# First chunk of a state-space block: D * u as products with a diagonal, modulation products one ahead of their sums, row statistics and transposes tile by tile, the feed-forward gate moved into the loop

## The chip, the core and the metric

One NeuronCore of a Trainium2 chip runs the kernel. The metric is the device time of one execution in microseconds. The core has five instruction queues that run in parallel and wait for one another through semaphores: TensorE (PE: matrix products and transposes into PSUM), VectorE (DVE), ScalarE (ACT), GpSimd (POOL) and SyncE (SP, which here issues all the DMAs). Each queue runs its own instructions strictly in the order in which the program wrote them.

## The reference

Two blocks follow each other on x (2 batches, 2048 rows, 512 features), both in float32. Only the first one is touched here. It is an S5 state-space layer with modulation by a condition t, followed by a feed-forward layer:

```python
mod = t @ Wm + bm
shift_a, scale_a, gate_a, shift_ff, scale_ff, gate_ff = jnp.split(mod, 6, axis=-1)
y_mod = _ln(y) * (1 + scale_a[:, None]) + shift_a[:, None]
a_y = _s5(y_mod, ...)       # 2 * Re(C xs) + D_diag * u, xs[l] = Lam_bar * xs[l-1] + B_bar u[l]
y = y + gate_a[:, None] * a_y
scale_c, shift_c = jnp.split(t @ Wc + bc, 2, axis=-1)
y_norm = _ln(y) * (1 + scale_c[:, None]) + shift_c[:, None]
y_mod = y_norm * (1 + scale_ff[:, None]) + shift_ff[:, None]
h = jax.nn.gelu(y_mod @ W1 + b1)
return y + gate_ff[:, None] * (h @ W2 + b2)
```

The second block is a style layer norm with softmax attention (16 heads) and a residual. It takes most of the time and stays as it is.

## The kernel before, in words

x is worked in chunks of 512 rows: 2 batches by 4 chunks. A chunk is four tiles of 128 rows (rows on the partitions, 512 features along them). For products over features it is transposed into four pieces of 128 features by 512 rows. Every float32 product is two instructions on TensorE; a transpose is one.

The order of the work is written out by hand; nothing reorders it. There is a prologue, which does everything of the first chunk up to its feed-forward product (L243 to L601), and then a loop over the chunks (L628). Each turn of the loop runs the feed-forward products of one chunk (`ff_first` L484 and `ff_second` L495, 16 steps f), and a table `due[f, half]` hangs the other work between them: the state-space part of the next chunk and the attention projections of the one before. In the first turn two steps stand in that table beside these: `rest_of_mod` (L616, two more modulation vectors) and `rows_of_biases` (L624).

The prologue, in order:

- SP loads x, the weights of the modulation vectors (1 MB each, `load_mod` L215), B (`br`, `bi`), C (`c2_re`, `c2_im`), and the feed-forward weights in quarters.
- VectorE computes the constants of the state-space layer on one column (128x1): `exp_full` (L286) for the step and for the decay, sine and cosine, and then the scaled B (`bb_re`, `bb_im`, L377). Most are short operations that depend on the one before. POOL multiplies C by 2 and -2 (L381).
- `modulate` (L220) makes a modulation vector: TensorE multiplies the condition with the weights in four column groups (tile `pq`, L226), ScalarE copies the result (`quarters`, L230), and TensorE sums the four groups with small products (L233). For several vectors this chain is done one after another: product, copy, sum. `modulated` (L235) adds the biases on VectorE.
- `normalised` (L392) takes the layer norm of the chunk: statistics of all four tiles, scale, then four normalising operations. `to_features` (L145) transposes the normalised chunk by feature piece, four tiles each, and ScalarE applies scale and shift.
- `phases` (L341) builds the rotation table by doubling on VectorE. `s5_in` (L415) multiplies with B (`pu`), `s5_turn` (L425) rotates, `s5_scan` (L437) runs the recurrence (two scans) and rotates back into `h_re`, `h_im`; in the last two POOL does one operation and three operations.
- `s5_direct` (L456) adds D * u, times the gate, on POOL: u is the normalised chunk with a scale and a shift, so the rows `r_scale` and `r_shift` multiply and are added, three operations a tile. `gate_row` (L387) spreads such a vector over all partitions by TensorE and a copy.
- `s5_out` (L464): for each tile the two products with C (`pa`), the gate on VectorE (`gated`), the addition to x on POOL.
- `gate_row` for the feed-forward gate and its bias, then the second layer norm (`ff_norm` L476, in which POOL also adds the gated bias b2), and its transposes (`ff_features` L481).

PSUM has eight banks: two buffers with the tag `ph`, four banks with the tag `po`, and two banks that `ones` gives out in turn.

Of the kernel before, what the change touches and what calls it, by code (L numbers as in the profile page):

```python
# [39 lines left out]
def tile_s5_block_then_sln_attention(  # L40
# [87 lines left out]
    def ln_stats(src, n, mean, rstd):  # L128

        mv = small.tile([P, n, 2], F32, name="ln_mv", tag=f"ln_mv{n}")  # L130
        for t in range(n):
            st = small.tile([P, 6], F32, name="ln_st", tag="ln_st", bufs=4)
            nc.vector.bn_stats(st, src[:, t, :])
            nc.vector.bn_aggr(mv[:, t, :], st)
        v = small.tile([P, n], F32, name="ln_v", tag=f"ln_v{n}")
        nc.vector.tensor_scalar(v, mv[:, :, 1], EPS, None, ALU.add)
        nc.vector.tensor_copy(mean, mv[:, :, 0])
        rsqrt(v, rstd, n)
# [81 lines left out]
    def modulate(pm, *ms, first=0):  # L220

        for i, m in enumerate(ms, first):
            w = wms.pop(m)
            pq = ps1.tile([P, D], F32, name="pq", tag="ph")
            for k in range(KC):
                nc.tensor.matmul(  # L226
                    pq[32 * k : 32 * k + 32, :], cond_q[:, k, :], w[:, k, :], start=True, stop=True
                )
            quarters = work1.tile([P, D], F32, name="quarters", tag="hid", bufs=3)
            nc.scalar.copy(quarters, pq)  # L230
            for f in range(KC):
                at = slice((i * KC + f) * NB, (i * KC + f + 1) * NB)
                nc.tensor.matmul(pm[:, at], quarters[:, f * P : (f + 1) * P], four, start=True, stop=True)  # L233

# [14 lines left out]
    c2_im = s5c.tile([P, D], F32, name="c2_im")  # L249
    for dst, src in ((br, b_re), (bi, b_im), (c2_re, c_reT), (c2_im, c_imT)):  # L250
        nc.sync.dma_start(dst, src)
# [4 lines left out]
    load_mod(SHIFT_C, xlate, "x1")  # L256
    load_mod(GATE_F, xpool, "x2")
    w1_sb = wts.tile([P, KC, FC * P], F32, name="w1_sb")
    w2_sb = wts.tile([P, FC, D], F32, name="w2_sb")
    for q in range(4):  # L260
        f = FC // 4
        cols = slice(q * f * P, (q + 1) * f * P)
        nc.sync.dma_start(w1_sb[:, :, cols], w1[:, cols].rearrange("(k p) f -> p k f", p=P))
        nc.sync.dma_start(w2_sb[:, q * f : (q + 1) * f, :], w2[cols, :].rearrange("(c p) e -> p c e", p=P))


    def col(name):
        return s5c.tile([P, 1], F32, name=name)

    def ts(dst, a, s1, s2, op0, op1=None):  # L270
        if op1 is None:
            nc.vector.tensor_scalar(dst, a, s1, None, op0)
        else:
            nc.vector.tensor_scalar(dst, a, s1, s2, op0, op1)

    def stt(dst, a, s, b, op0, op1):
        nc.vector.scalar_tensor_tensor(dst, a, s, b, op0, op1)

    def poly(dst, r, cs):

        ts(dst, r, cs[-1], None, ALU.mult)
        for c in reversed(cs[1:-1]):
            stt(dst, dst, c, r, ALU.add, ALU.mult)
        ts(dst, dst, cs[0], None, ALU.add)

    def exp_full(dst, a, n):  # L286

        q, k, r = col(f"{n}q"), col(f"{n}k"), col(f"{n}r")
        ts(q, a, 88.0, -87.0, ALU.min, ALU.max)
        ts(k, q, LOG2E, ROUND, ALU.mult, ALU.add)  # L290
        ts(k, k, ROUND, None, ALU.subtract)
        stt(r, k, -LN2_HI, q, ALU.mult, ALU.add)
        stt(r, k, -LN2_LO, r, ALU.mult, ALU.add)
        poly(dst, r, [1.0, 1.0, 1 / 2, 1 / 6, 1 / 24, 1 / 120, 1 / 720, 1 / 5040])
        e = s5c.tile([P, 1], I32, name=f"{n}e")
        ts(e, k, 127.0, 8388608.0, ALU.add, ALU.mult)
        nc.vector.tensor_mul(dst, dst, e.bitcast(F32))

# [4 lines left out]
    nc.vector.tensor_mul(theta, l_im, dt)  # L303
    exp_full(decay, damp, "dc")

# [70 lines left out]
    bb_im = s5w.tile([P, D], F32, name="bb_im", tag="m5")  # L376
    ts(bb_re, br, k_re, None, ALU.mult)  # L377
    stt(bb_re, bi, neg_im, bb_re, ALU.mult, ALU.add)
    ts(bb_im, br, k_im, None, ALU.mult)
    stt(bb_im, bi, k_re, bb_im, ALU.mult, ALU.add)  # L380
# [27 lines left out]
    def tag_of(b, c):  # L408
        return f"f{index[b, c] % 2}"
# [14 lines left out]

    def s5_turn(b, c):  # L425

        bu = bus.pop((b, c))
        m = [s5w.tile([P, CH], F32, name=f"m{i}") for i in range(6)]
        nc.vector.tensor_mul(m[0], bu[0], t_re)
        nc.vector.tensor_mul(m[3], bu[0], t_im)  # L430
        nc.vector.tensor_mul(m[1], bu[1], t_im)
        nc.vector.tensor_mul(m[2], bu[1], t_re)  # L432
        nc.vector.tensor_add(m[0], m[0], m[1])
        nc.gpsimd.tensor_tensor(m[2], m[2], m[3], ALU.subtract)  # L434
        bus[b, c] = m

    def s5_scan(b, c):  # L437
        m = bus.pop((b, c))
# [5 lines left out]
        nc.vector.tensor_mul(m[0], m[1], t_re)  # L444
        nc.gpsimd.tensor_mul(m[4], m[1], t_im)
        nc.vector.tensor_mul(m[2], m[3], t_im)
        nc.gpsimd.tensor_mul(m[5], m[3], t_re)
        nc.vector.tensor_sub(h_re, m[0], m[2])
        nc.gpsimd.tensor_tensor(h_im, m[4], m[5], ALU.add)
        for i, h in enumerate((h_re, h_im)):  # L450
# [103 lines left out]
    def s5_gates(b):  # L554
        gate_row(b, "r_scale", r_scale)
        gate_row(b, "r_shift", r_shift)
        gate_row(b, "gate_a", mod[:, GATE_A])

# [3 lines left out]
    for dst, src in ((bT_re, bb_re), (bT_im, bb_im)):  # L562
# [3 lines left out]
        nc.scalar.copy(dst.rearrange("p k q -> p (k q)"), pb)  # L566
    modulate(spare[:, 1], GATE_A)
    normalised(*start)
    modulated(spare[:, 0], SHIFT_A, SCALE_A)
    nc.vector.tensor_scalar(u_scale, mod[:, SCALE_A], 1.0, None, ALU.add)  # L570
    for k in range(KC):
        s5_features(*start, k)
    modulated(spare[:, 1], GATE_A)
    nc.vector.tensor_mul(r_shift, mod[:, GATE_A], per_feature(V_D))
    nc.vector.tensor_mul(r_scale, r_shift, u_scale)
    nc.vector.tensor_mul(r_shift, r_shift, mod[:, SHIFT_A])
    phases()
    later = (SHIFT_F, SCALE_F, SCALE_C, SHIFT_C, GATE_F)
    modulate(spare[:, 2], *later[:1])
    s5_gates(start[0])  # L580
    s5_in(*start)
    modulate(spare[:, 2], *later[1:], first=1)
    s5_direct(*start, (0, 1))
    s5_turn(*start)
    s5_direct(*start, (2,))
    s5_scan(*start)
    s5_direct(*start, (3,))
    modulated(spare[:, 2], *later)
    tmp = small.tile([P, KC, NB], F32, name="zs")
# [3 lines left out]
    nc.vector.tensor_add(z_shift, z_shift, mod[:, SHIFT_F])  # L593
    nc.vector.tensor_mul(gate_b2, mod[:, GATE_F], per_feature(V_B2))
    for t in range(TT):
        s5_out(*start, t)
    gate_row(start[0], "gb2", gate_b2)
    gate_row(start[0], "gate_f", mod[:, GATE_F])
    ff_norm(*start)
    for k in range(KC):  # L600
        ff_features(*start, k)  # L601

# [10 lines left out]
    bv_row = wlate.tile([P, D], F32, name="bv_row")  # L613
    bp_row = wlate.tile([P, D], F32, name="bp_row")

    def rest_of_mod():  # L616
# [11 lines left out]
    for i, now in enumerate(order):  # L628
# [8 lines left out]

        if i == 0:
            due[1, 1].append((rest_of_mod,))
            due[2, 1].append((rows_of_biases,))  # L640
        if behind:
# [682 lines left out]
```

## Time and profile before

| what | us |
|---|---|
| median of 3 runs | 3458.43 (3457.08 to 3461.29) |
| the profiled execution, its own time | 3459.56 |
| its span, first to last instruction | 3457.8 |
| prologue, to the first product of the feed-forward (L487) | 80.45 |
| from there to the end of the first eight products of its third step | 24.6 (80.45 to 105.02) |
| TensorE busy in the prologue | 56.8 of 80.45 |
| TensorE busy from 117 to 860 us (rest of the feed-forward stretch read) | 742.7 of 742.9 |

Busy shares of the whole span mix stages with different limits, so the prologue is read by its chain of waits and by its timeline. In a row of the timeline stand start, length, engine, line, operation, the tile written, the tiles read, and how many instructions were merged; a bracket gives the idle time of the engine before it and what ended that time. The row of a window also names the TensorE clock that was granted (1.00 is the full clock), and the share of time in which the DMA engines were busy.

### The profile page before, as it was taken

The page shows a single profiled execution, that of the slowest core. Times are in us where ns is not written, and L with a number is a line of the kernel's source. Part 1 is how long each engine was busy: PE and PEld are TensorE (multiplying, and loading weights), DVE is VectorE, ACT ScalarE, POOL GpSimd, SP SyncE. Part 2 cuts the span into 40 slices and gives each one's busy share as a digit, 9 for nine tenths or more (in the row PEclk, how much of TensorE's full clock was granted, in tenths as well). Part 3 has the DMA queues.
Part 4 walks back from the last instruction along what each step waited for, and adds up shares of the span by engine and source line. Part 5 has one row for each costly group of instructions (what it writes and reads, how often), then busy time and mean ns, then how long its engine had stood idle before and what let it go on. Part 6 is the DMA issues. An engine that isn't in the chain of part 4 may idle for free.

```text
span 3457.8 us, 34348 instructions
## 1 busy us (share of the span) xinstructions
PE 3335.5 (96%) x11764; PEld 1508.3 (44%) x11764; DVE 2151.7 (62%) x2976; ACT 1939.8 (56%) x2208; POOL 2137.8 (62%) x1162
## 2 busy tenths in 40 slices
PE   7999999999999999999999999999999999999997
PEld 4444444444444444444444444444444444444432
DVE  6232323232322310688888888888888888888885
ACT  2111111111111111398999999999888888888963
POOL 4133131313131310289898989998898989899986
PEclk8999999999999999999999999999999999999999
DMA  8001111111110112432223222223234233233233
GB/s 304 1 31 43 43 43 43 43 43 43 43 43 31 43 37 61 121 77 67 58 62 72 66 67 54 72 67 75 70 81 96 65 87 85 71 85 78 61 97 115
DMA packets 201396, 237.06 MB, mean 69 GB/s; under 512 B 89544, under 2 KB 118728, under 8 KB 197126
## 3 DMA queue, kind: packets, MB, share of 16 engines
q1 hardware_dynamic: 201222, 234.87, 24.5%
q8 instruction: 93, 1.52, 0.2%
q14 instruction: 81, 0.66, 0.1%
HBM read 166.77 MB, written 67.76 MB: 68 GB/s over the span
## 4 chain that ended last, share of the span: by engine, by line
PE 73%; DVE 14%; ACT 8%; issue 2%; DMA 1%; POOL 1%; SPq 0%; DVEq 0%; ACTq 0%; POOLq 0%
PE o L834 15%; PE ph L487 13%; PE po L500 13%; PE s L754 10%; DVE run L770 10%; PE pk L530 6%; ACT x L765 4%; PE pv L542 3%; PE m L779 3%; PE py L905 2%; PE pt_run L790 2%; ACT pT L824 2%; ACT x L824 2%; PE pu L421 2%; PE pt_tf L149 1%
## 5 line engine op out<-in xcount | busy, mean ns | idle before, releaser
L813 POOL TENSOR_TENSOR x<-x,shift 128x1024 f32<-128x1024 f32 x704 | 1653.8, 2387 | 153.6 <-DMA shift<-flat 104.6
L765 ACT COPY x<-s 128x1024 f32<-128x1024 f32 x704 | 692.4, 1012 | 213.0 <-PE s L754 211.9
L770 DVE TENSOR_TENSOR run<-s,run 128x1024 f32<-128x1024 f32 x576 | 702.9, 1220 | 73.6 <-ACT x L765 50.2
L824 ACT ACTIVATE x<-x 128x1024 f32<-128x1024 f32 x704 | 739.8, 1060 | 11.9 <-POOL x L813 11.6
L754 PE MATMUL s<-qs,ks 128*128 128x512 f32 x2048 | 669.5, 421 | 51.3 <-DVE run L770 45.2
L834 PE MATMUL o<-x,v 128*64 128x512 f32 x2816 | 718.4, 612 | 0.0
L487 PE MATMUL ph<-fT,w_sb 128*128 128x512 f32 x1024 | 463.5, 597 | 0.0
L500 PE MATMUL po<-w_sb,hid 128*128 128x512 f32 x1024 | 460.3, 592 | 0.0
L754 PEld LDWEIGHTS s<-qs,ks 128*128 128x128 f32 x2048 | 334.4, 189 | 275.4 <-DVE run L770 149.7
L819 DVE TENSOR_TENSOR pT<-s,shift 128x1024 f32<-128x1024 f32 x320 | 389.5, 1217 | 85.1 <-PE s L754 85.1
L784 DVE TENSOR_REDUCE top<-m 128x1 f32<-128x640 f32 x512 | 417.4, 815 | 9.8 <-PE m L779 7.1
L491 ACT ACTIVATE hid<-ph,vec 128x512 f32<-128x512 f32 x128 | 88.0, 687 | 595.9 <-PE ph L487 595.9
L824 ACT ACTIVATE pT<-pT 128x1024 f32<-128x1024 f32 x320 | 339.4, 1061 | 50.2 <-DVE pT L819 50.2
L158 DVE SCALAR_TENSOR_TENSOR lo<-pk,vec,hi 128x512 fp32r<-128x512 f32 x64 | 48.0, 751 | 494.4 <-ACT hi L157 494.4
L834 PE MATMUL o<-pT,v 128*64 128x512 f32 x1280 | 330.5, 595 | 7.9 <-ACT pT L824 7.9
L487 PEld LDWEIGHTS ph<-fT,w_sb 128*128 128x128 f32 x1024 | 193.3, 192 | 228.9 <-issue 228.9
L834 PEld LDWEIGHTS o<-x,v 128*64 128x64 f32 x2816 | 157.1, 135 | 310.4 <-issue 191.4
L434 POOL TENSOR_TENSOR m<-m,m 128x512 f32<-128x512 f32 x8 | 13.1, 1643 | 449.7 <-DVE m L432 449.7
L500 PEld LDWEIGHTS po<-w_sb,hid 128*128 128x128 f32 x1024 | 190.7, 190 | 221.5 <-issue 221.5
L779 PE MATMUL m<-ks,qs 128*128 128x320 f32 x1024 | 256.6, 332 | 17.3 <-DVE top L784 15.5
L157 ACT ACTIVATE hi<-pk,vec 128x512 fp32r<-128x512 f32 x64 | 44.0, 687 | 383.3 <-PE pk L530 383.3
L510 POOL TENSOR_TENSOR x<-x,gated 128x512 f32<-128x512 f32 x32 | 39.6, 1269 | 354.4 <-DVE gated L509 354.4
(253 smaller groups left out, 2774.6 us busy)
## 6 DMA issues: line engine op xcount, KB each, us to landing
ks<-kd SPq DMA_DIRECT2D x128, 256.0 KB
qs<-qd SPq DMA_DIRECT2D x512, 64.0 KB
shift<-flat SPq DMA_DIRECT2D x64, 512.0 KB
x<-in_x SPq DMA_DIRECT2D x8, 1024.0 KB
w_sb<-in_w SPq DMA_DIRECT2D x8, 1024.0 KB
x<-x SPq DMA_DIRECT2D x8, 1024.0 KB
kd<-hi SPq DMA_DIRECT2D x32, 256.0 KB
kd<-lo SPq DMA_DIRECT2D x32, 256.0 KB
```

Source lines behind the costliest of these rows:

```text
L487: nc.tensor.matmul(ph, w1_sb[:, k, f * P : (f + 1) * P], fts[b, c][:, k, :], start=k == 0, stop=k == KC - 1)
L500: nc.tensor.matmul(pos[b, c][:, t, :], hid[:, t * P : (t + 1) * P], w2_sb[:, f, :], start=f == 0, stop=f == FC - 1,)
L530: nc.tensor.matmul(pk, w[:, k, g * P : (g + 1) * P], hT[:, k, :], start=k == 0, stop=k == KC - 1)
L754: nc.tensor.matmul(s[:, e, :], kst[pair_of[n], e][:, kt * P : (kt + 1) * P], qst[n][:, e, :], start=True, stop=True,)
L765: nc.scalar.copy(x, s)
L770: nc.vector.tensor_tensor(runs[n], s, kept[n, 0] if kt == 1 else runs[n], ALU.max)
L779: nc.tensor.matmul(m[:, i, :YW], qst[n][:, e, t * P : (t + 1) * P], kst[pair_of[n], e][:, k : k + YW], start=True, stop=True,)
L784: nc.vector.tensor_reduce(tops[n][:, j, 0:1], m[:, :, :YW], AX.XY, ALU.max, negate=True)
L813: nc.gpsimd.tensor_tensor(x, x, shifts[n], ALU.add)
L819: nc.vector.tensor_tensor(x, s, shifts[n], ALU.add)
L824: nc.scalar.activation(x, x, AF.Exp)
L834: nc.tensor.matmul(outs[n][64 * e : 64 * e + 64, :], v[:, kt, e : e + 2, :], x[:, e, :], start=first, stop=final,)
```

## The change

- The exponential of the decay (15 operations) moves from VectorE to POOL. The operations that took a scalar and a column are written as one tensor-scalar operation each.
- `br` times a column goes from VectorE to ScalarE (two operations), ahead of everything else that ScalarE does.
- `modulate` issues the product of the next vector before the sum of the last one. The vectors are grouped anew: SHIFT_A and SCALE_A as before; GATE_A, SHIFT_F and SCALE_F together; SCALE_C and SHIFT_C together; GATE_F goes into the loop.
- The loads of C move behind the weights of the modulation vectors, the one of GATE_F behind the first two quarters of the feed-forward weights.
- In the first chunk the operations that POOL had in `s5_turn` and `s5_scan` are VectorE's. Later chunks keep them on POOL.
- In the first chunk `s5_direct` is gone: D * u is added in PSUM, by 16 products of u with diagonal tiles (`direct`, made by POOL), ahead of the products with C. The rows `r_scale` and `r_shift`, which later chunks still need, move into the loop.
- The statistics of the second layer norm follow each tile's addition, the last tile's addition is VectorE's, and the transposes go tile by tile into one four-bank PSUM tile.
- Three steps hang in the loop's first turn: `gate_of_feed_forward` at (1, 0), with the vector GATE_F, its two rows and POOL's addition of the gated bias; `rest_of_mod` at (1, 1), as before; the rows of `s5_gates` at (2, 0).

```diff
@@ modulate
+        def sums(i, quarters):
+            for f in range(KC):
+                at = slice((i * KC + f) * NB, (i * KC + f + 1) * NB)
+                nc.tensor.matmul(pm[:, at], quarters[:, f * P : (f + 1) * P], four, start=True, stop=True)
...
             nc.scalar.copy(quarters, pq)
-            for f in range(KC):
-                at = slice((i * KC + f) * NB, (i * KC + f + 1) * NB)
-                nc.tensor.matmul(pm[:, at], quarters[:, f * P : (f + 1) * P], four, start=True, stop=True)
+            if behind:
+                sums(*behind)
+            behind = i, quarters
+        sums(*behind)
@@ loads
-    for dst, src in ((br, b_re), (bi, b_im), (c2_re, c_reT), (c2_im, c_imT)):
+    for dst, src in ((br, b_re), (bi, b_im)):
...
-    load_mod(GATE_F, xpool, "x2")
+    for dst, src in ((c2_re, c_reT), (c2_im, c_imT)):
+        nc.sync.dma_start(dst, src)
...
+        if q == 0:
+            load_mod(GATE_F, xpool, "x2")
@@ constants
-    exp_full(decay, damp, "dc")
+    exp_full(decay, damp, "dc", nc.gpsimd)
...
-    ts(bb_re, br, k_re, None, ALU.mult)
+    nc.scalar.activation(bb_re, br, AF.Identity, scale=k_re)
+    nc.scalar.activation(bb_im, br, AF.Identity, scale=k_im)
     stt(bb_re, bi, neg_im, bb_re, ALU.mult, ALU.add)
-    ts(bb_im, br, k_im, None, ALU.mult)
@@ first chunk
-    modulate(spare[:, 1], GATE_A)
+    modulate(spare[:, 1], GATE_A, SHIFT_F, SCALE_F)
...
+    uT = fts[start]
+    s5_in(*start)
+    modulated(spare[:, 1], GATE_A, SHIFT_F, SCALE_F)
     phases()
...
-    s5_gates(start[0])
-    s5_in(*start)
-    modulate(spare[:, 2], *later[1:], first=1)
-    s5_direct(*start, (0, 1))
-    s5_turn(*start)
-    s5_direct(*start, (2,))
-    s5_scan(*start)
-    s5_direct(*start, (3,))
+    modulate(spare[:, 2], SCALE_C, SHIFT_C)
+    s5_turn(*start, nc.vector)
+    gate_row(start[0], "gate_a", mod[:, GATE_A])
+    s5_scan(*start, nc.vector)
+
+    direct = work1.tile([P, KC, P], F32, name="direct", tag="hi")
+    for k in range(KC):
+        nc.gpsimd.tensor_scalar(direct[:, k, :], ident, vec[:, V_D + k : V_D + k + 1], None, ALU.mult)
+    pas = [ps1.tile([P, CH], F32, name="pa_s", tag="ph") for _ in range(2)]
+    pas += [ones.tile([P, CH], F32, name="pa") for _ in range(2)]
+    for t, pa in enumerate(pas):
+        cols = slice(t * P, (t + 1) * P)
+        for k in range(KC):
+            nc.tensor.matmul(
+                pa[:, k * P : (k + 1) * P], uT[:, k, cols], direct[:, k, :], start=k == 0, stop=False
+            )
...
+    for t, pa in enumerate(pas):
+        cols = slice(t * P, (t + 1) * P)
+        nc.tensor.matmul(pa, h_re[:, cols], c2_re, start=False, stop=False)
+        nc.tensor.matmul(pa, h_im[:, cols], c2_im, start=False, stop=True)
+    for t, pa in enumerate(pas):
+        g = work1.tile([P, D], F32, name="gated")
+        nc.vector.tensor_mul(g, pa, gate[start[0], "gate_a"])
+        if t:
+            ln_row(xc, t - 1, mv)
+        (nc.gpsimd if t < TT - 1 else nc.vector).tensor_tensor(xc[:, t, :], xc[:, t, :], g, ALU.add)
+    ln_row(xc, TT - 1, mv)
+    ln_scale(mv, TT, mean, rstd)
...
     for t in range(TT):
-        s5_out(*start, t)
-    gate_row(start[0], "gb2", gate_b2)
-    gate_row(start[0], "gate_f", mod[:, GATE_F])
-    ff_norm(*start)
+        normalise(xn[:, t, :], xc[:, t, :], mean, rstd, t)
+        for k in range(KC):
+            nc.tensor.transpose(pt[:, k, t * P : (t + 1) * P], xn[:, t, k * P : (k + 1) * P], ident)
     for k in range(KC):
-        ff_features(*start, k)
+        nc.scalar.activation(
+            fts[start][:, k, :], pt[:, k, :], AF.Identity,
+            bias=z_shift[:, k, start[0] : start[0] + 1], scale=z_scale[:, k, start[0] : start[0] + 1],
+        )
@@ the loop's first turn
+    def gate_of_feed_forward():
+        pm = ones.tile([P, KC * NB], F32, name="pg")
+        modulate(pm, GATE_F)
+        modulated(pm, GATE_F)
+        nc.vector.tensor_mul(gate_b2, mod[:, GATE_F], per_feature(V_B2))
+        gate_row(start[0], "gb2", gate_b2)
+        gate_row(start[0], "gate_f", mod[:, GATE_F])
+        for t in range(TT):
+            nc.gpsimd.tensor_tensor(xc[:, t, :], xc[:, t, :], gate[start[0], "gb2"], ALU.add)
...
         if i == 0:
+            due[1, 0].append((gate_of_feed_forward,))
             due[1, 1].append((rest_of_mod,))
+            due[2, 0].append((s5_gates, start[0]))
             due[2, 1].append((rows_of_biases,))
```

## The prediction

> **What bounds the kernel now.** I read the shares per engine and the chain of waits first: they ask whether a microsecond won at the front reaches the end.
>
> ```profile
> PE 3335.5 (96%) x11764; PEld 1508.3 (44%) x11764; DVE 2151.7 (62%) x2976; ACT 1939.8 (56%) x2208; POOL 2137.8 (62%) x1162
> PE 73%; DVE 14%; ACT 8%; issue 2%; DMA 1%; POOL 1%; SPq 0%; DVEq 0%; ACTq 0%; POOLq 0%
> ```
>
> TensorE is busy 96% of the span. In the feed-forward stretch from 117 to 860 us it is busy 742.7 of 742.9 us: no slack is left there to absorb an earlier start, so what the front gains passes on. The diff touches the front, up to the first feed-forward product (L487, 80.45 us), and three steps inside that loop's first turns. So I read the chain of the first 120 us next (start, length, what).
>
> ```profile
> 35.08 6.87 PE pu L421 x16
> 41.95 1.04 PE pq L226 x8
> ...
> 51.00 1.87 PE spare L233 x8
> 52.87 1.91 PE pq L226 x8
> 54.85 0.59 ACT quarters L230
> 55.49 1.86 PE spare L233 x8
> 57.35 1.92 PE pa L469 x2
> ...
> 66.41 0.87 PE pa L470 x2
> ...
> 67.38 0.69 DVE gated L472
> 68.07 0.61 DVE ln_st L133
> ...
> 73.48 3.82 DVE xn L141 x4
> ...
> 80.66 8.41 PE ph L487 x16
> ```
>
> TensorE sets the order to 67.3: four modulation vectors from 41.95 to 57.35, each a product (pq), a wait for ScalarE's copy, a sum (spare); then the output products pa. After that VectorE sets it. The last scan value, h_im, is there at 55.65 (its last copy is at 55.68), so VectorE and POOL trail TensorE closely.
>
> Third, the clock by half microseconds, since one product costs 1.04 or 1.9 us by it (columns: window, length, PE busy, clock, DMA share, GB/s).
>
> ```profile
> 28.50:29.00 0.50, 0.50 (x4) 0.50 1.04 385
> 29.00:29.50 0.50, 0.50 (x8) 0.99 1.06 389
> ...
> 46.00:46.50 0.50, 0.00 (x0) 0.58 1.06 393
> 46.50:47.00 0.50, 0.49 (x3) 0.50 1.04 385
> ```
>
> The changes, at 25.6, 29.0, 46.1, 63.1, 73.4, 83.6 and 97.3, lie whole multiples of 3.41 us apart: the clock is decided per window. My reading of the windows: dense products for about 85% of one raise it, under some 45% drop it, and the tiny sums (128x2) hardly count.
>
> Fourth, what POOL does to VectorE.
>
> ```profile
> 33.95 1.28 POOL L460 TENSOR_TENSOR xn<-xn,r_scale 128x512 f32<-128x512 f32 x1 [16.00 <-ACT r_scale L168]
> 34.01 1.36 DVE L272 TENSOR_SCALAR tb<-t_re,t_im 128x256 f32<-128x256 f32 x1
> 43.19 0.68 DVE L433 TENSOR_TENSOR m<-m,m 128x512 f32<-128x512 f32 x1
> 43.91 4.32 DVE L442 TENSOR_TENSOR_SCAN m<-decay,m 128x512 f32<-128x512 f32 x2
> 48.15 1.69 DVE L444 TENSOR_TENSOR m<-m,t_re 128x512 f32<-128x512 f32 x1
> ```
>
> A VectorE operation on two tensors takes 0.68 us alone (0.60 apart) and about 1.7 beside POOL's; the scan 1.20 to 2.22 over all its uses.
>
> **The change, stage by stage**, on the clock windows of this trace.
>
> *To 19 us: nothing.* The decay exponential leaves VectorE for POOL, -2.63 us (5.42 to 8.05); POOL's c2 scaling leaves this stretch, about -0.5 (k_re took 0.66 instead of 0.16). k_re is then ready near 12.7, but br lands about 13.35 (an estimate: c_re landed at 14.69, two 256 KB loads later at 390 GB/s). ScalarE makes bb_re and bb_im, 13.35 to 14.55; VectorE's two remaining operations end at 15.3 (19.0 before). But these two stand on ScalarE ahead of the first quarters copy, which moves from 11.96 to 14.6; the second product, now one ahead, waits for its megabyte until 12.65 (9.96, where the first landed, + 2.7 for 1 MB at 390 GB/s). The sums run 15.25 to 18.95, against 18.89 before. One-ahead is worth nothing here.
>
> The 15 dependent POOL operations are shown nowhere in this form. The nearest row:
>
> ```profile
> 3447.49 0.20 POOL L1090 TENSOR_TENSOR c<-scale 128x4 f32<-128x4 f32 x1
> 3447.77 0.20 POOL L1091 TENSOR_TENSOR c<-c,v 128x4 f32<-128x4 f32 x1
> ```
>
> Start to start 0.29, hence 4.3 us, done at 9.7; needed by about 11.6, that is 0.41 us each. Bounds: 0.20 (busy time alone) costs nothing; 0.60 (twice the row) costs 15 x 0.19 = 2.9. I take 0.29, nothing: VectorE's other constants cover it.
>
> *19 to 38.5: +3.4.* Transposes of bb end at 20.9. Three products and three sums, warm from about 22.2: first product 1.6, then 2 x 1.05 and 3 x 1.05, with copies hidden by one-ahead and only issue gaps: 27.75. Their weights, 1 MB each behind bi's 14.0, land at 16.7, 19.4 and 22.1, in time. The layer norm on VectorE is done at 22.8 (7.4 us after 15.3), so the 16 transposes begin at 27.75 and end at 30.8 by ScalarE's four 0.7 us passes; the clock falls at 29.0 after the sums and rises at 32.4. Input products pu (16 instructions): 30.85 to 32.4 at half clock, 1.8 of them at 0.855, then 14.2 at 0.43 = 6.1, ending 38.5 against 41.95. The r_scale and r_shift rows (16 of 24, 1.9 us) no longer stand ahead of them.
>
> Here a rule speaks against the change. The Trainium skill, "TensorE: Matmul & The Clock Gate", Part 4, says that transposes do not count as activity for the full clock. The row is against it: from 25.6 to 29.0 TensorE ran nothing but L149 transposes, and at 29.0 the clock rose. By the rule pu would stay at half speed one window longer: 3.41 / 2 = 1.7 us off the sum below, 10.9 in place of 12.6. I take the row.
>
> *38.5 to 48.7: +5.2.* Before, 15.4 us from 41.95 to 57.35 for four vectors. Now two: 4 x 1.06 = 4.25, to 42.75. That window holds little dense work, so the clock falls as at 46.1: the gate_a row 1.75, then 32 diagonal products (16 in two passes) at 0.107 warm, as in L164's 0.86 for 8, twice that cold: 1.55 cold and 2.65 warm. TensorE is ready at 48.7 (47.0 if the clock holds, 51.5 if all is cold). VectorE: phases start at 28.3 behind the later modulated, 8.1 us without POOL beside the wide steps, +0.5 for c2, end 36.9; turn waits for pu's imaginary half, 38.7 + 4 x 0.61 = 41.15; scans 2 x 1.25; six products 3.65: h_im at 47.3. POOL's c2 scaling moves behind five loads and finishes near 31.6; nothing needs it before 47. Moving POOL's share to VectorE costs 4 x 0.6 there and frees both from each other. TensorE decides, by 1.4 us.
>
> *pa, 48.7 to 55.6: +3.0.* 16 at 0.43 = 6.9 us; before 9.9, half of it at half clock. gated, row statistics and POOL's add (0.6, 0.8, 1.27) fit in each tile's 1.72.
>
> *Tail: +4.7.* Before 67.28 to 80.45 = 13.2. Now after the last pa: gated 0.7, one row's statistics 0.85, add on VectorE 0.7, last row 0.85, scale 2.3 (L134 to L141), four xn 1.92 (as at 24.43; 3.82 beside POOL's bias adds), transposes and ScalarE's first pass 1.2 = 8.5. Loop starts at 64.1: 16.3 us earlier.
>
> *Inside the loop: -3.7.* Gate of feed-forward: product 1.06, copy 0.76, sums 1.05, VectorE 0.55, two rows 1.75 = 5.2; everything on TensorE behind it, po first, waits for it. ScalarE's gelu of the second piece (0.69) stands ahead of the copy and ends within the product. Two rows of s5_gates: 1.75. Against it, rest_of_mod took 92.43 to 98.6 and left the next eight ph at half clock until 105.02: 9.2 us beyond ph's own 3.43. One ahead it is 4.2 us, too short to drop the clock for most window positions: 5.3 with 0.38 x 3. The same for the gate step, 0.2 x 3 = 0.6. Sum 5.8 + 1.75 + 5.3 - 9.2 = 3.7. POOL's bias adds, 5.1 us, find POOL idle from 80 to 154; uncovered they would add 1.9 to the tail, as before.
>
> SP's queue: GATE_F goes behind two weight quarters, landing near 37, needed at 73 (14.0 + 8.5 MB at 2.7). x1, wk and the rest wait for modulation products that are now earlier.
>
> **Sum** 3.4 + 5.2 + 3.0 + 4.7 - 3.7 = 12.6. Other window positions can only add cold stretches to the gate row and triple; estimate -0.8. Gain 11.8. On the profiled execution (span 3457.8, 1.76 around it, 3459.56) that is 3447.8; it lies 1.1 above the median 3458.43, which gives 3446.6. I say **3447**. Under 0.2% (7 us) is what a measurement cannot tell from no change.
>
> **The rivals.**
> - *The clock takes it back* (13%). Bad window positions: triple +1.5, pu +1.7, gate row and diagonals +1.5, ph behind both loop steps +3.5: gain about 4, 3454. For: the clock fell twice beside such steps. Against: they are shorter now.
> - *Clock holds throughout* (15%). pu one us earlier, diagonals 1.7 earlier but VectorE's 47.3 decides (+1.4), loop +1.7: gain 16, 3442.
> - *Nothing arrives* (5%): a later wait absorbs it, 3457. Against: 742.7 of 742.9.
> - *POOL's exponential becomes the bound* (5%). At L297 for decay: ScalarE's bb_re waits for k_re, the quarters copies wait behind it, TensorE's sums behind those. Price 15 x (p - 0.41) us: the gain is gone at p = 1.2, slower by 7 us at p = 1.66: 3465. For: operations with a pointer scalar on POOL are not in the trace. Against: 0.29.
>
> **How the numbers follow.** The forecast has 62%, its own range 3443 to 3451. Faster: 62 + 15 = 77%; same: 13 + 5 = 18%; slower 5%. The range 3441 to 3454 takes in the holding clock and the bad one; outside lie mostly the last two rivals and errors of my schedule.
>
> **What would show it.** Right: the first ph near 64 us; pa beginning within 1 us of h_im and of the last diagonal product; scans near 1.25 us, L444 near 0.68; xn 0.5 each. Wrong: decay's last POOL operation after 11.6 and the first quarters copy after 14.6; the transposes behind the triple later than 30; a half clock during pa or through the second ph; po's first product more than 6 us behind the second ph.

## The result, and the profile after

The changed kernel takes 3445.73 us (median of 6 runs, 3444.56 to 3452.13), the kernel before 3459.61 us in the same comparison (6 runs, 3457.08 to 3465.84). The ratio is 0.9961, 95% interval 0.9948 to 0.9974: 13.9 us less. The forecast was 3447 us, about 11.8 us less.

First the engines' shares and the chain by engine, on the page of the changed kernel.

```profile
PE 3325.6 (97%) x11796; PEld 1506.7 (44%) x11796; DVE 2141.9 (62%) x2964; ACT 1940.9 (56%) x2210; POOL 2119.3 (62%) x1164
PE 73%; DVE 13%; ACT 9%; DMA 2%; issue 2%; POOL 1%; SPq 1%; DVEq 0%; ACTq 0%; POOLq 0%
```

As before, TensorE sets the time; it has 32 instructions more (the diagonal products). Next the chain of waits of its first 100 us (start, length, what).

```profile
13.41 1.28 ACT L393
14.71 0.72 ACT bb_re L393
...
20.14 1.81 PE pb L582 x8
21.95 3.49 PE pq L238 x16
...
33.58 8.05 PE pu L437 x16
41.63 1.85 PE pq L238 x16
43.49 1.88 PE spare L231 x16
...
48.15 1.79 PE pa L607 x16
49.94 0.86 PE pa_s L623 x2
...
56.84 0.69 DVE gated L627
...
62.68 3.67 PE pt_s L639 x16
66.42 0.79 ACT fT L641
67.25 7.13 PE ph L503 x16
74.39 1.04 PE pq L238 x8
...
86.94 3.54 PE ph L503 x8
...
97.48 3.44 PE ph L503 x8
```

The last row is the mark that all runs below are read by: the first feed-forward product of the loop's fourth step. By then everything that the change touches is done, the steps moved into the loop included. In the kernel before it is this row:

```profile
110.24 3.44 PE ph L487 x8
```

It stands at 110.24 before and at 97.48 after: **12.76 us** earlier, against 12.6 in the forecast's sum. The first attention products (tile m) start at 1398.7 and 1386.0, 12.7 apart: what is gained at the mark arrives undiminished 1300 us later. From there to the end it takes 2059.1 us before and 2057.3 after, and between 2056.7 and 2062.5 over all the profiles below, so that a total holds a few microseconds that no part of the change has made.

| where | before | forecast | after |
|---|---|---|---|
| transposes of bb begin | 18.76 | 18.95 | 20.00 |
| pu ends | 41.95 | 38.5 | 41.63 |
| first pa | 57.35 | 48.7 | 49.94 |
| last pa ends | 67.28 | 55.6 | 56.82 |
| first ph | 80.45 | 64.1 | 67.25 |
| mark, ph of the fourth step | 110.24 | 97.6 | 97.48 |

The total is right, the way there is not: the prologue gained 13.2 us instead of 16.3, and the loop gave back 0.4 instead of 3.7.

### The profile page after: what moved, and what is told of

The parts are those of the page before. It is cut to its first block, busy times and chain, and to the rows that moved or that the text cites. A ratio compares the mean times of both kernels' runs of the same rounds, so it can differ in the third digit from the quotient of the medians.

```text
span 3443.3 us, 34398 instructions
## 1 busy us (share of the span) xinstructions
PE 3325.6 (97%) x11796; PEld 1506.7 (44%) x11796; DVE 2141.9 (62%) x2964; ACT 1940.9 (56%) x2210; POOL 2119.3 (62%) x1164
## 4 chain that ended last, share of the span: by engine, by line
PE 73%; DVE 13%; ACT 9%; DMA 2%; issue 2%; POOL 1%; SPq 1%; DVEq 0%; ACTq 0%; POOLq 0%
PE o L892 15%; PE ph L503 13%; PE po L516 13%; PE s L812 10%; DVE run L828 9%; PE pk L546 6%; ACT x L823 4%; PE pv L558 3%; PE m L837 3%; PE py L963 2%; PE pt_run L848 2%; ACT pT L882 2%; ACT x L882 2%; PE pu L437 2%; PE pt_tf L155 1%
```

## The experiments

Beside each total stands the ratio to the kernel before, timed on the same chip. Totals that differ by less than 3 us can't be told apart by a handful of runs; the mark comes from one profiled execution of each.

### The yardstick: the changed kernel once more

> The changed kernel once more, as a yardstick on the same chip for the runs beside it: 3444 to 3448 us, the first feed-forward product at 66 to 69 us, the fourth step at 96.5 to 99.

Measured: 3448.22 us, ratio 0.9964 (0.9951 to 0.9976), first ph 67.12, mark 97.35. The mark repeats within 0.13 us, the median within 2.5 us. That the mark repeats so closely is luck, as the runs below show: in six executions TensorE has the same work up to the end of pu (these two, the run with the clock held, the two with POOL's share, and the one with the gate behind the output products), and pu ends at 41.63, 41.60, 40.61, 39.49, 39.23 and 38.47. The changes of the clock lie elsewhere in each execution. A difference of less than 3 us between the marks of two profiles is therefore not shown to come from the edit.

### One-ahead undone

```diff
-            if behind:
-                sums(*behind)
-            behind = i, quarters
-        sums(*behind)
+            sums(i, quarters)
```

> The changed kernel with each modulation vector's sums issued directly behind its own product again, the one-ahead order undone everywhere, all else kept. Theory: nothing in the first pair (the quarters copies wait behind bb on ScalarE in both), two exposed copies of about 0.75 us each in the group of three, one in the group of two and one in the loop's pair, and more half clock: first feed-forward product 2.5 to 4 us later, near 70 to 71 us, the loop's pair of vectors 4.5 us or more and not 3.7, total 3 to 6 us longer than the changed kernel. Rival, VectorE's rotation and scan set the start of the output products: the first feed-forward product is less than 1 us later.

Measured: 3458.65 us, ratio 0.9998 (0.9989 to 1.0006), first ph 75.00, mark 110.23. The whole gain is gone, four times my lower bound and twice the upper. The chain of this run:

```profile
16.64 1.87 PE spare L231 x8
18.51 1.91 PE pq L238 x8
20.44 0.60 ACT quarters L242
21.08 1.86 PE spare L231 x8
22.94 1.81 PE pb L579 x8
...
40.19 7.27 PE pu L434 x16
...
95.46 1.86 PE pm L231 x8
97.32 5.90 PE ph L500 x8
```

In the first pair the second product now stands behind the first sums, which wait for ScalarE until 16.6; bb's transposes start 2.8 us later (22.94 against 20.14). The group of three costs 3.8 us more, the pair behind pu 1.9, the loop's pair 2.6, and the eight ph behind that pair fall to half clock, 5.90 in place of 3.54 us. pu gives 0.8 back by its clock.

### One-ahead alone, on the kernel before

```diff
+        def sums(i, quarters):
...
+            if behind:
+                sums(*behind)
+            behind = i, quarters
+        sums(*behind)
```

> The kernel before with the one-ahead order of the modulation products alone (groups, loads, POOL and everything else as before). Undone alone in the changed kernel this order cost 12.7 us at the first product of the loop's fourth step (110.23 against 97.48), as much as the whole change gained. Two-chain theory: TensorE's chain of modulation and clock and VectorE's chain of rotation table, scan and POOL meet at the first output product within 0.1 to 2 us, in both kernels, so that each part undone alone gives back nearly all, and each part alone gains little: in the kernel before h_im is ready at 55.65 and the first output product starts at 57.2, so the prologue gains no more than about 2 us plus what the clock makes of the output products (up to 3), and the loop's pair of vectors and the half clock behind it gain 3 to 5: the first product of the fourth step 4 to 9 us earlier than 110.24, total 4 to 9 us shorter than before. Rival, the one-ahead order by itself is the change's gain: 11 to 14 us shorter than before.

Measured: 3452.43 us, ratio 0.9977 (0.9968 to 0.9986), 8.2 us shorter than before; first ph 78.42, mark 101.81. So alone it gains 8.4 us at the mark, and only 2.0 of these in the prologue. TensorE is through with its vectors at 50.8, and then it waits, as the timeline of this run shows.

```profile
46.10 2.19 POOL L467 TENSOR_TENSOR xn<-xn,r_scale 128x512 f32<-128x512 f32 x1
48.25 2.18 POOL L468 TENSOR_TENSOR x<-x,r_shift 128x512 f32<-128x512 f32 x1
50.51 1.59 POOL L469 TENSOR_TENSOR x<-x,xn 128x512 f32<-128x512 f32 x1
52.06 1.71 POOL L452 TENSOR_TENSOR m<-m,t_im 128x512 f32<-128x512 f32 x1
54.46 2.04 PE L476 MATMUL pa<-c_re,m 128*128 128x512 f32 x2 [3.69 <-DVE m L455]
56.83 2.08 PE L477 MATMUL pa<-c_im,m 128*128 128x512 f32 x2 [0.32 <-POOL m L456]
```

POOL's three operations for D * u stand ahead of its share of the scan. TensorE's first product waits 3.7 us for VectorE's h_re, its second another 0.3 us for POOL's h_im. Two chains meet at pa: TensorE's (modulation and clock) and the one of VectorE and POOL. Shortening one uncovers the other. That is why one-ahead is worth 8.4 us alone (2.0 in the prologue), and 12.75 us when it is taken away last (7.75 in the prologue).

### D * u back on POOL

```diff
+    gate_row(start[0], "r_scale", r_scale)
+    gate_row(start[0], "r_shift", r_shift)
+    s5_in(*start)
     phases()
+    s5_direct(*start)
...
-            nc.tensor.matmul(
-                pa[:, k * P : (k + 1) * P], uT[:, k, cols], direct[:, k, :], start=k == 0, stop=False
-            )
...
-            due[2, 0].append((s5_gates, start[0]))
```

> The changed kernel with D * u done on POOL again (12 operations on 128x512 with the two rows made ahead of the input products) and without the diagonal products; the rows of the loop's third step go with it. Theory: TensorE loses 3.6 us of diagonal products but has two rows of 1 us each (or 1.8 at half clock) ahead of the input products; VectorE is disturbed by POOL in the wide steps of the rotation table and in scan and rotation, 13.7 us from the imaginary input product to h_im before the change against 8.4: first feed-forward product 4 to 6 us later, near 72 us, the loop 1.8 us shorter without the two rows, the first product of its fourth step near 100.5 us (97.48 in the changed kernel), total 2 to 4 us longer. Rival, TensorE sets this stage and the POOL work is hidden: no change within 1 us or faster by the 1.6 us of TensorE's work.

Measured: 3459.58 us, ratio 0.9996 (0.9987 to 1.0004), first ph 77.55, mark 105.93: 8.45 us later than the changed kernel, where I had said 3. The timeline, VectorE and POOL:

```profile
40.05 1.32 POOL L476 TENSOR_TENSOR xn<-xn,r_scale 128x512 f32<-128x512 f32 x1
40.16 1.35 DVE L293 SCALAR_TENSOR_TENSOR t_im<-t_im,t_re,tb 128x128 f32<-128x128 f32 x1
44.07 1.50 DVE L293 SCALAR_TENSOR_TENSOR t_re<-t_im,neg,ta 128x256 f32<-128x256 f32 x1
```

and the same VectorE operation in the changed kernel:

```profile
37.41 0.34 DVE L293 SCALAR_TENSOR_TENSOR t_im<-t_im,t_re,tb 128x128 f32<-128x128 f32 x1
```

The operation that takes 0.34 us on 128 columns alone takes 1.35 beside POOL: it ends at 41.5, 0.1 us behind POOL's. The rotation table ends at 46.9, in the changed kernel at 39.2, and scan and rotation are slower too. I had costed the contention by the wide steps alone; it takes hold of those on 128 columns as well. Only 0.9 us of the delay is a later start of the table, behind the steps for the two rows.

### POOL's share of the first chunk's rotation and scan, twice

```diff
-    s5_turn(*start, nc.vector)
+    s5_turn(*start)
...
-    s5_scan(*start, nc.vector)
+    s5_scan(*start)
```

> The changed kernel with the four operations of the first chunk's rotation and scan back on POOL, all else kept. Later chunks take 9.7 us from the imaginary input product to h_im with POOL's help (153.2 to 162.9 before the change); the changed kernel takes 8.4 us without it (41.6 to 50.0), and TensorE is ready at 49.94. Theory: h_im about 1.3 us later, the first feed-forward product near 68.6 us (67.25 in the changed kernel), total 1 to 2 us longer. Rival, the separation of the two engines was the main gain: 4 us or more longer. Rival, POOL's help counts for more than its disturbance: faster.

Measured: 3456.37 us (20 runs, one of them far off at 4787 us, for no reason that is known), ratio 0.9984 (0.9978 to 0.9991), first ph 73.29, mark 105.65: 8.2 us later, not 1.3. This run looked like the rival. POOL's timeline says otherwise.

```profile
47.53 1.59 POOL L465 TENSOR_TENSOR m<-m,m 128x512 f32<-128x512 f32 x1
49.12 2.77 POOL L601 TENSOR_SCALAR direct<-ident,vec 128x128 f32<-128x128 f32 x4
50.19 3.96 PE L607 MATMUL pa_s<-direct,fT 128*128 128x128 f32 x16 [5.98 <-POOL direct L601]
```

h_im is there at 49.1, where the theory had it, in a run whose pu ended earlier. But the diagonal tiles stand behind the rotation on POOL's queue, and TensorE waits 6 us for them. The edit had moved them without my saying so. So the run was made again with the tiles first:

```diff
+    for k in range(KC):
+        nc.gpsimd.tensor_scalar(direct[:, k, :], ident, vec[:, V_D + k : V_D + k + 1], None, ALU.mult)
     modulate(spare[:, 2], SCALE_C, SHIFT_C)
-    s5_turn(*start, nc.vector)
+    s5_turn(*start)
```

> As the run with POOL's share of rotation and scan, but POOL makes the diagonal tiles before its first rotation operation. In that run the tiles stood on POOL's queue behind the rotation and were made from 49.1 us on, which kept TensorE's diagonal products waiting until 50.2 (6 us idle): 8.2 us later at the fourth step. Theory: with the tiles first only h_im's own delay is left, 9.7 us behind the imaginary input product in place of 8.4: the first feed-forward product 1 to 2 us later than 67.25, the fourth step 1 to 2 us later than 97.48, total 1 to 3 us longer than the changed kernel. Rival, sharing with POOL is itself what costs: 5 us or more longer, as in the run before.

Measured: 3447.41 us, ratio 0.9963 (0.9950 to 0.9977), first ph 67.86, mark 100.40. The prologue loses 0.6 us. The mark loses 2.9, because the 16 first ph take 9.45 us in place of 7.13: in this run they start at half clock, which lasts beyond 72 us. So sharing with POOL is not what cost 8.2 us, and in the total the run can't be told from the changed kernel. But sharing is not free. Here VectorE rotates from 38.85 on and the last of h_re and h_im is there at 50.21, 11.4 us later; in the run with the gate behind the output products, where POOL has no share, this takes from 38.38 to 47.30, 8.9 us. That pa still starts at 50.25, only 0.3 us later than in the changed kernel, comes from pu, which ended 2.4 us earlier in this run.

### The decay exponential back on VectorE

```diff
-    exp_full(decay, damp, "dc", nc.gpsimd)
+    exp_full(decay, damp, "dc")
```

> The changed kernel with the decay exponential back on VectorE. The prediction's stage to 19 us held that br, landing near 13.4, hides it entirely up to the point where k_re comes later than br. k_re ends at 13.32 in the changed kernel, with the table load of ScalarE to 14.7 behind br. Theory: k_re 2.3 to 2.6 us later, near 15.8, hence bb_re at about 15.9 and not 14.7: the first quarters copy and the first feed-forward product 1.1 to 1.3 us later. If POOL's exponential had been the limit, the kernel would become faster here. If it had been hidden by br as predicted, nothing changes.

Measured: 3448.49 us, ratio 0.9964 (0.9951 to 0.9977), first ph 67.43, mark 97.66. bb_re starts at 16.46 and not 14.71, and bb's transposes are 1.75 us later (21.89). By pu the difference is 0.14 us: the group of three runs 7.8 us in the changed kernel and 6.7 here, since its first products meet the full clock sooner, and the chain goes over VectorE's scale of the first chunk. POOL's exponential was ready at 10.77, 1.1 us before it was needed. The move is worth 1.75 us at 20 us and nothing measurable at the mark, where I had expected 1.1 to 1.3.

### The table load first

```diff
     nc.gpsimd.memset(cond_q, 0.0)
+    warm = const.tile([P, 1], F32, name="warm")
+    nc.gpsimd.memset(warm, 0.0)
+    nc.scalar.activation(warm, warm, AF.Identity, scale=1.0)
```

> The changed kernel with one activation of a single column (Identity) put ahead of everything on ScalarE, so that the table load of 1.28 us, which stands at 13.41 us in front of bb_re in the changed kernel, is done in the first 3 us. Theory: that load is on the path from br to the first quarters copy, so bb_re starts at 13.4 and not 14.7, the first quarters copy near 14.7 and not 15.95, and the first feed-forward product 1.3 us earlier, near 66 us (67.25 in the changed kernel), total 1 to 2 us shorter. Rival, the loads of the modulation weights set the pace of this stretch: the copy moves but the third modulation product still waits for its megabyte, and the first feed-forward product stays within 0.3 us of 67.25.

In the kernel before, the load is this row of the timeline; here it stands at 0.71 us again:

```profile
0.71 1.28 ACT L230 ACT_TABLE_LOAD   x1 [0.71 <-PEq L1315]
```

Measured: 3445.34 us, ratio 0.9954 (0.9938 to 0.9971), first ph 65.16, mark 97.40. The prologue is 2.1 us shorter (1.1 of it at the transposes of bb, 0.9 because pu runs at a higher clock in this run), the mark is where it was. The windows of this run, around the first ph (window, length, PE busy, clock, DMA share, GB/s):

```profile
66.00:66.50 0.50, 0.50 (x2) 0.50 0.97 365
69.00:69.50 0.50, 0.50 (x2) 0.76 0.20 74
```

and of the changed kernel:

```profile
65.50:66.00 0.50, 0.50 (x5) 0.50 1.06 389
66.00:66.50 0.50, 0.34 (x2) 0.82 1.04 385
66.50:67.00 0.50, 0.00 (x0) 1.00 1.15 410
```

In the changed kernel the window up to 66.2 is full of transposes, the clock rises, and ph at 67.25 runs at full clock, 7.13 us. In this run the transposes lie across a window's edge (60.57 to 64.26), the clock rises near 69.2, and ph takes 9.14. What the prologue gained, the first ph lost again.

### The clock held over the row statistics

```diff
+    for _ in range(6):
+        nc.tensor.matmul(pt[:, 0, :], ident, c2_re, start=True, stop=True)
     xns[start] = xn = xnp.tile([P, TT, D], F32, name="xn")
```

> The changed kernel with six dummy products of 128x512 (identity times C, into the PSUM bank that the transposes overwrite afterwards) between the last output product and the transposes, where TensorE stands idle for 5.9 us. Theory: the full clock is then held through the row statistics; the 16 transposes take about 1.9 to 2.2 us and not 3.67, VectorE's four normalising operations (1.92 us) pace them, ScalarE's first pass starts 1.5 us earlier and the first feed-forward product is near 65.6 us. Rival, the transposes take their time from latency or from waits and not from the clock: the 16 take 3.6 us again and nothing moves. [...]

The six products are extra work; their output is overwritten. Measured: 3446.88 us, ratio 0.9961 (0.9946 to 0.9975), first ph 64.61, mark 94.83. The chain:

```profile
61.66 2.04 PE pt_s L641 x16
63.78 0.79 ACT fT L643
64.61 7.13 PE ph L503 x16
```

The 16 transposes take 2.04 us and not 3.67: half clock was their price. The mark is 2.65 us earlier, of which 1.0 comes from an earlier pu in this run, ahead of the edit. The total does not show it.

### A warm start

```diff
+    for _ in range(30):
+        nc.tensor.matmul(spare[:, 3, :P], ident, ident, start=True, stop=True)
-    modulate(spare[:, 0], SHIFT_A, SCALE_A)
+    modulate(spare[:, 0], SHIFT_A, SCALE_A, fill=4)
```

`fill` puts four more of these extra products behind each of the two modulation products.

> The changed kernel with 30 dummy products of 128x128 ahead of the first modulation product, in the 8.5 us in which TensorE waits for the first megabyte, and four more behind each of the first two products. Theory: the full clock at the start makes the first two products 1.06 and not 1.94 us, the first 16 sums 1.9 to 2.1 and not 3.58, the transposes of bb 0.9 and not 1.81, so that the group of three begins near 19.5 us and not 21.95: first feed-forward product 2 to 4 us earlier, total 2 to 4 us shorter. Rival, as the run with the early table load showed, a stretch that starts earlier meets the clock windows elsewhere: the prologue is shorter by 2 us or more but the first product of the fourth step is not earlier than 97. Rival, the stretch is set by the loads (SCALE_F lands near 22): less than 1 us.

Measured: 3446.41 us, ratio 0.9954 (0.9939 to 0.9969), first ph 66.30, mark 96.52: 1.0 us earlier, less than two profiles can tell apart. The products take 1.06 us as foreseen, but the sums still wait for ScalarE until 16.48. The 16 sums take 2.57 us, and by the transposes of bb the half clock is back (1.81 us for eight).

### The feed-forward gate behind the output products

```diff
+    pg = ps1.tile([P, KC, CH], F32, name="pg", tag="po", bufs=1)
+    modulate(pg[:, 0, :], GATE_F)
...
     ln_row(xc, TT - 1, mv)
+    modulated(pg[:, 0, :], GATE_F)
+    nc.vector.tensor_mul(gate_b2, mod[:, GATE_F], per_feature(V_B2))
+    gate_row(start[0], "gb2", gate_b2)
+    gate_row(start[0], "gate_f", mod[:, GATE_F])
     ln_scale(mv, TT, mean, rstd)
```

The same steps leave `gate_of_feed_forward`; POOL's additions stay there.

> The changed kernel with the vector GATE_F and its two rows taken out of the loop's second step (5.4 us on TensorE there, 74.39 to 79.77) and put behind the output products, where TensorE is idle for 5.9 us; POOL's additions of the gated bias stay in the loop. Theory: the work is covered by VectorE's row statistics, up to 1 us of it delays the transposes: first feed-forward product between 66 and 68.5 us, the first product of the fourth step near 92.5 us and not 97.48, total 4 to 5 us shorter. Rival, the two rows wait for VectorE's biases and push the transposes back by their whole 2 us, and the clock stays low: the first feed-forward product near 70 us and the gain below 2.5 us.

Measured: 3442.84 us, ratio 0.9945 (0.9929 to 0.9962), first ph 65.33, mark 90.18, 7.3 us earlier than the changed kernel. The chain and, last, a row of the timeline:

```profile
59.89 3.83 DVE xn L147 x4
63.76 0.67 PE pt_s L645 x4
...
65.33 7.13 PE ph L503 x16
72.47 3.43 PE po L516 x8
```

```profile
60.75 5.30 POOL L670 TENSOR_TENSOR x<-x,gb 128x512 f32<-128x512 f32 x4 [5.90 <-ACT gb L174]
```

TensorE did the gate while it would have been idle, so the loop's 5.4 us are gone. The row of the gated bias is ready early now, and POOL begins its additions beside VectorE's normalising: 3.83 us for four in place of 1.92. That the first ph is 1.9 us earlier all the same is not the edit's work: pa began 2.6 us earlier in this run (47.35), since pu ended at 38.47. Of the 7.3 us the edit explains 4.7, the loop's 5.4 less 0.7 lost in the tail.

### All that the runs point to

```diff
+    nc.scalar.activation(warm, warm, AF.Identity, scale=1.0)
...
+    modulate(spare[:, 0], SHIFT_A, SCALE_A, fill=4)
     nc.scalar.activation(bb_re, br, AF.Identity, scale=k_re)
...
+    modulate(pg[:, 0, :], GATE_F)
+    nc.tensor.matmul(pg[:, 1, :], ident, c2_re, start=True, stop=True)
...
+        g = gates.tile([P, D], F32, name=f"{name}_{start[0]}", tag=name)
+        nc.scalar.copy(g, pr)
```

The last two lines stand behind ScalarE's passes of the transposed pieces, so that POOL's additions start after VectorE's normalising. The 30 extra products of the warm start are in it too.

> The changed kernel with all that the runs point to: the table load first, the first pair of modulation products ahead of bb on ScalarE, dummy products that hold the clock before and in the first pair, GATE_F's vector and rows behind the output products with one more dummy, and the copies of these rows behind the transposed pieces on ScalarE, so that POOL's bias additions do not meet VectorE's normalising operations (3.83 us in the run with the gate in the tail, 1.92 without). Theory: transposes of bb near 17 us and not 20.1, the group of three limited by SCALE_F's load near 22, transposes of the first chunk near 26 and not 29.8, first feed-forward product 60 to 63 us, the first product of the fourth step 85 to 88 us (97.48 in the changed kernel, 90.18 with the gate in the tail), total 8 to 12 us shorter than the changed kernel. Rival, the loads and the clock windows take the front's part back: not faster than the run with the gate in the tail by more than 2 us.

Measured: **3439.80 us** (3439.41 to 3440.38), ratio 0.9940 (0.9926 to 0.9953), first ph 65.58, mark 90.42. Its median is the lowest of all here, and it is faster than both kernels. But its mark is that of the run before, and by the ratios (0.9940 and 0.9945) the two can't be told apart: the rival. The timeline of TensorE shows where the front's gain went.

```profile
16.37 0.63 PE L589 MATMUL pb<-ident,bb_re 128*128 128x128 f32 x4
17.37 1.07 PE L241 MATMUL pq<-wm,cond_q 128*32 128x512 f32 x8
20.67 1.06 PE L241 MATMUL pq<-wm,cond_q 128*32 128x512 f32 x8 [2.23 <-DMA wm<-in_w_mod]
23.38 1.93 PE L241 MATMUL pq<-wm,cond_q 128*32 128x512 f32 x8
25.24 3.58 PE L234 MATMUL spare<-four,quarters 128*128 128x2 f32 x16
```

bb's transposes begin 3.6 us earlier than in the changed kernel. Then TensorE waits for SHIFT_F's megabyte until 20.67, and around these gaps the clock falls (at 21.9): the third product and the sums run at half. At 28.7 the lead is down to 0.9 us. In the tail the two rows are at half clock (3.56 us for 16).

## Why the prediction was right, point by point

- **"To 19 us: nothing."** Wrong by 1.2 us. The missing term: ScalarE's first instruction is now bb_re, and its table load of 1.28 us comes at 13.41 with it, in front of the quarters copies. In the kernel before it lay at 0.71 and cost nothing; nothing in the diff says "load". Of the two signs of being wrong that I had named together, the first quarters copy came after 14.6 (at 15.95), by the load; POOL's last operation came before 11.6 (it was done at 10.77). The step's other sentence, that one-ahead is worth nothing there, is wrong too: the second product would else stand behind the late sums, 2.8 us by the run that undid it. I had compared the end times of two kernels and read their equality as no effect.
- **"19 to 38.5: +3.4"** was +0.3 at pu's end. 1.1 us came with the late start. The group of three took 7.8 us and not 6.85, for its first 16 instructions took 3.49, most of it at half clock; the transposes of the chunk took 3.8 and not 3.1, and pu 8.05 and not 7.65. The windows fell otherwise than forecast, and where they fall is chance: in the run with the gate behind the output products, with the same work on TensorE up to there, pu ended at 38.47.
- **The rule on transposes** (the Trainium skill, "TensorE: Matmul & The Clock Gate", Part 4). The row decided rightly. In the changed kernel the window from 62.8 to 66.2 holds only transposes, and the clock rises at its end; the run with the early table load shows the counter-case, with half a window of them and no rise.
- **The reading of the windows**, that products for about 85% of one raise the clock and under some 45% drop it. The upper share does not hold. Three windows of 3.41 us at half clock held transposes alone. In the run with one-ahead undone, 2.85 us of them from 71.2 to 74.6 raised the clock; in the kernel before, 2.85 us from 76.8 to 80.2 did not, nor did 3.17 us from 24.9 to 28.3 in the run with one-ahead alone. The lower share is nearer: with the sums left out, 1.3 us from 42.7 to 46.1 before let the clock fall, and 1.7 us from 42.3 to 45.7 in the changed kernel did not.
- **"38.5 to 48.7"**, 10.2 us, was 8.3. Two products back to back take 1.85 and not 2.12, two groups of sums 1.88, and the clock did not fall. TensorE decided, but not by 1.4 us over h_im: the diagonal products end at 49.94, h_re is there at 49.4 and h_im at 50.0, which the second product of the first pair first needs at 50.80.
- **pa**: 6.9 us, as forecast.
- **The tail**, 8.5 us, was 10.4. I let VectorE's xn pace the transposes and costed the last batch at full clock. At half clock the 16 take 3.67, and ScalarE's first pass starts only behind the last of them. The run with the clock held took 2.04.
- **"Inside the loop: -3.7"** was -0.4. The gate step cost 5.38 (5.2 forecast) and the rows 1.78 (1.75). Mis-sized were the pair of vectors, 3.73 with nothing at half clock behind it (5.3), and the first 16 ph: 7.13 where I had left the 8.41 of before. The transposes of the new tail had raised the clock.

So the mechanism of most parts stood, the table load and the shares of the windows excepted, and the sum hit by luck: errors of 3 us in the front and 2 in the tail met gains of 2 behind pu and 3 in the loop. The 3 us of the front alone can come and go with the windows. By the runs, the gain is not additive: one-ahead undone costs 12.75 us at the mark, D * u undone 8.45, together more than the 12.76 that the change brought. Of the rivals, POOL's exponential did not become the bound (start to start 0.27 to 0.37 us, ready 1.1 us early). The clock did both: it gave some 3 us in the loop (1.3 in the first ph, 1.7 of half clock that I had allowed for and that did not come) and took 1.6 in the tail (3.67 against 2.04). Nothing was absorbed later: 12.7 us are left at the first attention product.

Not undone by a run of its own: the tail in tiles, the new groups of vectors, and GATE_F in the loop. What these are worth is read from the chain alone (2.7 us for the tail). Not tried: the group of three with its loads in another order, and the clock held through the loads' gaps of the last run.

## What to carry to other kernels

Where two chains meet at one wait, a part's worth is what it uncovers: cost each chain to the meeting point, and expect that undoing a part can cost more than the part gains alone (12.75 against 8.4 us here). Ahead of a moved operation look for what comes with it on its engine's queue: a table load in front of the first activation, tiles behind a rotation, a copy behind a scale. In a stretch of short products the clock is a term of its own, and where its windows lie differs from execution to execution (up to 3 us at the end of pu here). So cost each batch at both clocks, give the range a few microseconds for it, and don't read an edit's worth from two single profiles that differ by less.

## What the runs showed of the hardware

- The clock changes in steps of 3.41 us: in the changed kernel at 28.6, 35.5, 59.4 and 66.2, that is 2, 7 and 2 steps apart. Where the steps lie differs from execution to execution, and with it the end of the same TensorE work: 38.47 to 41.63 us.
- A window with nothing but transposes in it can raise the clock: at 66.2 in the changed kernel, at 29.0 in the kernel before.
- A prologue that is 2.1 us shorter can end at the same place: 16 products took 7.13 us or 9.14 us by where a window's edge lay.
- The table load carries the line of ScalarE's first operation, but need not run right ahead of it: at 0.71 us in the kernel before, 11 us ahead of the first copy, and at 13.41 us, behind the wait for B, in the changed kernel. With a small activation put first, which waits for no load, it ran at 0.71 us again.
- A VectorE operation on 128 columns took 0.34 us alone and 1.35 beside a POOL operation on two tensors: it ended 0.1 us after POOL's did.
- Short dependent POOL operations on one column took 0.19 to 0.23 us, those with a scalar from memory 0.27, and 0.27 to 0.37 from start to start.
